# Mixing as four 64x64 products: a fused four-layer image kernel on one core

## The chip, the cores and the metric

The kernel runs on one core of one Trainium2 chip. The metric is the device time of one execution in microseconds. A core has a matrix engine (PE, with its weight loads PEld), a vector engine (DVE), a scalar engine (ACT), a general engine (POOL), and a sync engine (SP) that here only issues transfers. Each engine runs its own instructions in order; between engines there are semaphores. Products write PSUM, [...]DVE and ACT read them from there.

## The reference, cut to what matters

The input `x` holds 16 images of 64 channels of 128 x 128 pixels in fp32. Four residual layers follow each other; `_gn` is a group norm over pairs of channels.

```python
# layer 0: gram matrix of an image's channels, applied to it, then a 1x1 convolution
xf = x.reshape(B, C, N)
gram = jnp.einsum('bcn,bdn->bcd', xf, xf) / N
y = jnp.einsum('bcd,bdn->bcn', gram, xf)
out = jnp.einsum('oc,bchw->bohw', conv_w, y.reshape(B, C, H, W))

x = x + _L0_conv_ref(_gn(x), L0_conv_conv_w)
x = x + _L1_conv_ref(_gn(x))               # |3x3 gradient in x| + |3x3 gradient in y|, per channel
x = x + _L2_conv_ref(_gn(x), L2_conv_W, L2_conv_b)   # temporal shift, 3x3 convolution
x = x + _L3_conv_ref(_gn(x), ...)          # binary 3x3, then 1x1, then a batch norm over all images
```

Layer 0 is linear in the pixels once the image's gram matrix is known: its result is a 64 x 64 matrix (called `A` below, with the residual and the norms' factors in it) times the image's 64 channels, plus a constant. The batch norm of layer 3 needs sums over all 16 images, so the last step comes after everything else.

## The kernel before

**Pieces.** An image is handled in 8 chunks (`NS`), one a step. A chunk is 8 rows (`R`) of the upper half of the image and the 8 rows that lie 64 below: partitions 0 to 63 are the 64 channels of the upper half's rows, partitions 64 to 127 the channels of the lower half's. Products take 4 rows (`CP`), 512 columns, at a time.

**Stages.** `Gram` (from line 464) reads an image with its rows across partitions (`load`, tile `xr`, 512 KB each), copies them on ACT into `xw` (`rows_to_columns`), and forms the gram matrix in 128 small products into `pg`; `gram_chain` turns it, in a chain of small DVE steps and products in the PSUM tile `bank`, into `abd` (128 x 128, with `A` twice on its diagonal and zeros elsewhere) and the coefficients `co`. `Front` (from line 513) is layers 0 and 1: `load` brings a chunk of `x`, `mix` multiplies it by `abd` into the bank `po`, `prepare` normalizes it on ACT into `xh`, `sobel` does the gradients on DVE, `store` writes the result to memory (`x2_d`). `Layer2` and `Layer3` read their rows back or from tiles; each has in every step six products into `one` and two times five (`own`) into the two halves of `two`. `own` needs a difference of rows `d`, which DVE makes, and a shifted copy of it `qd`, made by ACT copies for layer 3 and by two transfers on POOL's queue for layer 2.

**Order.** Every engine's instructions are kept in the order of the program (the wrapper `InOrder`, line 63). The main loop (line 978) runs over steps, and in a step over four quarters `q`; in each quarter first layer 3, then layer 2, then `Front`, then `Gram`, each with its own image and chunk: layer 3 starts at step 35 + 8b, layer 2 at 25 + 8b, `Front` at 15 + 8b for image b. So three images are in work at a time, and a fourth one's gram. At the end of a quarter every open chain goes one link further (`tick`). PE's order in a step is thus: layer 3's `one` and first `own` (eleven products), its second `own` (five), the first mixing, layer 2's `one` and first `own` (eleven), its second `own` (five), the second mixing. The gram's 128 products stand in three blocks at the end of the quarters named in `Gram.at` and `Gram.half`.

**The fill.** The grams of images 1 to 6 run twice as fast (`half`, four steps each, from step 12 on), those of images 7 to 15 at one image for eight steps (`at`), from step 38 on. `pace` (line 939) holds the step at which each starts. `xr` has three buffers.

**Mixing.** `small_product` (line 171) makes two products of 128 x 64, one for each half of the output partitions. `mix(i, 0)` stands in the second quarter, `mix(i, 1)` in the fourth, both into the single bank of the pool `ps_po`; the bank of the pool `ps_g` holds `pg`, and at the start of an image the product `pe` of the row beyond the halves' border. A product of fp32 shows in the profile as two matmuls, its two passes.

**The end.** From step 155 on, the buffers come free one by one and are filled with the stored results; after the batch norm's sums, only transfers with one ACT and one DVE operation for each 512 KB remain.

Of the kernel before, what the change touches and what calls it, by code (L numbers as in the profile page):

```python
# [10 lines left out]
F32 = mybir.dt.float32  # L11
# [4 lines left out]
B, C, H, W = 16, 64, 128, 128  # L16
P = 128
# [3 lines left out]
R = 8  # L21
NS = HH // R
EARLY = 3
CP = 4
# [84 lines left out]
def tile_kernel(ctx: ExitStack, tc: tile.TileContext, x, cw_h, w2_t, b2, wbin_t, w1_t, b1, gamma, beta, consts, out):  # L109
    nc = tc.nc  # L110
    pe, dve, act, sp, pool = (InOrder(tc, e) for e in (nc.tensor, nc.vector, nc.scalar, nc.sync, nc.gpsimd))
# [4 lines left out]
    small = ctx.enter_context(tc.tile_pool(name="small", bufs=4))  # L116
# [19 lines left out]
    def flat(ap):  # L136
        return ap.rearrange("p j w -> p (j w)")

    def halves(d, h, r0, n):

        v = d[0:C * HW].rearrange("(c r) -> c r", r=HW)
        return v[:, (h * HH + r0) * W:(h * HH + r0 + n) * W]
# [16 lines left out]
    ps_po = ctx.enter_context(tc.tile_pool(name="ps_po", bufs=1, space=PSUM))  # L159
    ps_g = ctx.enter_context(tc.tile_pool(name="ps_g", bufs=1, space=PSUM))  # L160
# [5 lines left out]
    def cols(o):  # L166
        return slice(o * C, (o + 1) * C)

    last = [1]

    def small_product(dst, wt, src):

        for o in (1 - last[0], last[0]):
            pe.matmul(dst[cols(o)], wt[:, cols(o)], src, start=True, stop=True)
        last[0] = o


    bank = ps_sm.tile([P, 512], F32, name="bank")
# [233 lines left out]
    def gram_product(pg, w):  # L412

        s = w % 2
        pe.matmul(
            pg[s * C:(s + 1) * C, :], xw[:, w // 2, 0:C, s], xw[:, w // 2, :, s],
            start=(w < 2), stop=(w >= W - 2),
        )
        last[0] = s

    def rows_to_columns(b, m, t):
        act.copy(
            xw[:, :, m * C // 8:(m + 1) * C // 8, :].rearrange("p w c t -> p c w t"),
            t.rearrange("p c (w t) -> p c w t", t=2),
        )
# [38 lines left out]
    class Gram:  # L464
        first, last = 0, NS + 1

        def __init__(self, b):
            self.b, self.xr, self.w = b, {}, 0

        def at(self, i, q):  # L470
            b = self.b
            if i < NS:
                if q == 0 and i != 1:
                    for m in range(i + (1 if i == 2 else 2) if i else 0, min(i + 3, NS)):
                        self.load(m)

                if q == 3 and i > 0:
                    for m in (0, 1) if i == 1 else (i,):
                        rows_to_columns(b, m, self.xr.pop(m))
                return  # L480
            n = 4 * (i - NS) + q

            self.part({0: 44, 2: 42, 4: 42}.get(n, 0))
            if n == 6:
                chains.append(gram_chain(b, self.pg))

        def part(self, n):
            if self.w == 0 and n:
                self.pg = ps_g.tile([P, CP, W], F32, tag="g", name=f"pg_{self.b}")[:, 0, 0:C + 1]
            for _ in range(n):  # L490
                gram_product(self.pg, self.w)
                self.w += 1

        def load(self, m):
            t = xin.tile([P, C // 8, W], F32, tag="xr", name=f"xr_{self.b}_{m}", bufs=3)
            sp.dma_start(t, x[self.b].rearrange("c h w -> h c w")[:, m * C // 8:(m + 1) * C // 8, :])
            self.xr[m] = t

        def half(self, r):

            if self.b > 1 and 6 <= r < 6 + NS:
                rows_to_columns(self.b, r - 6, self.xr.pop(r - 6))
            if self.b > 1 and 3 <= r < 3 + NS:
                self.load(r - 3)
            self.part({14: 44, 16: 42, 18: 42}.get(r - (self.b == 1), 0))
            if r - (self.b == 1) == 19:
                chains.append(gram_chain(self.b, self.pg))


    lo, hi = slice(0, C), slice(C, P)  # L510
    coefs2, coefs3 = {}, {}

    class Front:
        first, last = -3, NS

        def __init__(self, b):
            self.b, self.xs, self.po, self.x2 = b, {}, {}, {}
            self.st = stp.tile([P, 2, NS], F32, tag="st2", name=f"st2_{b}")

        def chunk(self, i):  # L520
# [5 lines left out]
        def load(self, i):  # L526
            b = self.b
            t = xin.tile([P, R, W], F32, tag="x", name=f"x_{b}_{i}")
            for h in range(2):
                sp.dma_start(flat(t[h * C:(h + 1) * C]), halves(x[b].rearrange("c h w -> (c h w)"), h, i * R, R))  # L530
            self.xs[i] = t

        def mix(self, i, g):
            if self.b == 0 and (i, g) in ((0, 1), (1, 0)):

                po = ps_two.tile([P, 2, CP, W], F32, tag="two", name=f"po_0_{i}_{g}")[:, 0]
            else:
                po = ps_po.tile([P, CP, W], F32, tag="po", name=f"po_{self.b}_{i}_{g}")
            small_product(po, self.abd, self.xs[i][:, g * CP:(g + 1) * CP, :])
            self.po[i, g] = po  # L540
# [9 lines left out]
        def at(self, i, q):  # L550
            b = self.b
            if q == 0:
                if i == -3:

                    self.xe = xin.tile([P, W], F32, tag="xe", name=f"xe_{b}", bufs=1)
                    sp.dma_start(self.xe[lo], x[b][:, HH, :])
                    sp.dma_start(self.xe[hi], x[b][:, HH - 1, :])
                    sp.dma_start(x2_d[b][0:W].rearrange("(p w) -> p w", p=1), w0[0:1, 0:W])
                if i + 3 < NS and i + 3 not in self.xs:
                    self.load(i + 3)  # L560
                if -1 <= i < NS - 1:
                    self.prepare(i + 1, 1)
                if 1 <= i:
                    self.store(i - 1)
                    act.activation(
                        junk.rearrange("p (j w) -> p j w", w=W), self.x2.pop(i - 1), AF.Square,
                        accum_out=self.st[:, 1, i - 1:i],
                    )
                if i == NS:
                    chains.append(coefficients(self.st, lambda co: coefs2.update({b: co}), b2_sb))  # L570
            if q == 1 and -2 <= i < NS - 2:
                if i == -2:
                    self.abd, self.co = lead.pop(b)
                    self.pe = ps_g.tile([P, CP, W], F32, tag="g", name=f"pe_{b}")[:, 0, :]
                    small_product(self.pe, self.abd, self.xe)
                self.mix(i + 2, 0)
            if q == 2:
                if i == -2:
                    nc.gpsimd.memset(self.chunk(0)[lo, 0, :], 0.0)
                    self.normalized(self.chunk(0)[hi, 0, 1:1 + W], self.pe[hi], hi)  # L580
                    self.pel = small.tile([P, W], F32, tag="pel", name=f"pel_{b}", bufs=1)
                    self.normalized(self.pel[lo], self.pe[lo], lo)
                if i == NS - 2:
                    nc.gpsimd.memset(self.chunk(NS - 1)[hi, R + 1, :], 0.0)
                    act.copy(self.chunk(NS - 1)[lo, R + 1, 1:1 + W], self.pel[lo])
            if 0 <= i < NS:
                self.sobel(i, q)
            if q == 2 and -2 <= i < NS - 2:
                self.prepare(i + 2, 0)
            if q == 3 and -2 <= i < NS - 2:  # L590
                self.mix(i + 2, 1)
                self.xs.pop(i + 2)

# [98 lines left out]
    class Layer2:  # L692
        first, last = -2, NS
# [146 lines left out]
    class Layer3:  # L840
        first, last = -1, NS
# [87 lines left out]
    live = {}  # L929
# [9 lines left out]
    pace = {}  # L939
    at = 12  # L940
    for b in range(1, B):

        pace[b] = at, 2 if b <= 2 * EARLY else 1
        at += NS // pace[b][1] + (2 if b == 2 * EARLY else 0)
    last_one = NS * (B - 1) + starts[0][1]
    steps = last_one + NS + 1

# [30 lines left out]
    for step in range(starts[2][1] - 2, steps):  # L978
        for q in range(4):
            for b in range(B):  # L980

                i = step - starts[2][1] - NS * b
# [10 lines left out]
            for b in range(1, B):  # L993
                at, n = pace[b]
                if n == 1:
                    run(Gram, b, step - at, q)
                elif 0 <= step - at <= 5:
                    live.setdefault((Gram, b), Gram(b)).half(4 * (step - at) + q)
# [110 lines left out]
```

## Time and profile before

| | |
|---|---|
| median of 3 runs | 2795.21 us (2790.94 to 2795.56) |
| the profiled execution | 2793.34 us, its span 2791.6 us |
| PE, DVE, ACT, POOL busy over the span | 80%, 79%, 76%, 31% |
| mean granted PE clock | 0.900 |
| steps of an image beside a gram, from one image's first `u<-xh` to the next's | 136.8 us |
| the same without a gram | 122.7 to 124.2 us |
| moved by transfers | 685.97 MB, 246 GB/s |

The span is the time from the first to the last instruction. In the page, a line of a group gives line, engine, operation, out<-in, count, then busy time, the mean of one in ns, and the idle time of the engine before them. Nearly all instructions carry the line 73, that of the wrapper, so groups are told apart by their tiles. In a timeline a line is start, length, engine, operation, tiles, shape and count, and in brackets the idle time before it with what ended it. The ends of matmuls are modelled: they overlap, and their starts say more than their lengths. Of a matmul 128*64 means 128 rows and 64 columns of the array.

### The profile page before, as it was taken

The page shows a single profiled execution, that of the slowest core. Times are in us where ns is not written, and L with a number is a line of the kernel's source. Part 1 is how long each engine was busy: PE and PEld are TensorE (multiplying, and loading weights), DVE is VectorE, ACT ScalarE, POOL GpSimd, SP SyncE. Part 2 cuts the span into 40 slices and gives each one's busy share as a digit, 9 for nine tenths or more (in the row PEclk, how much of TensorE's full clock was granted, in tenths as well). Part 3 has the DMA queues.
Part 4 walks back from the last instruction along what each step waited for, and adds up shares of the span by engine and source line. Part 5 has one row for each costly group of instructions (what it writes and reads, how often), then busy time and mean ns, then how long its engine had stood idle before and what let it go on. Part 6 is the DMA issues. An engine that isn't in the chain of part 4 may idle for free. (4 is left out here: it accounts for less than half of the span.)

```text
span 2791.6 us, 46444 instructions
## 1 busy us (share of the span) xinstructions
PE 2232.5 (80%) x14836; PEld 1097.1 (39%) x14836; DVE 2200.6 (79%) x3751; ACT 2115.3 (76%) x3177; POOL 865.2 (31%) x1350
## 2 busy tenths in 40 slices
PE   6578899999999999999999999999999995000000
PEld 4234444534454444353534343466666641000000
DVE  4998999898989898989898989999996435333332
ACT  4666789888888888888888888998997667333332
POOL 2054434342434343334343434444444310000000
PEclk8689999999999999999999999999999997555555
DMA  7789878888888888888888867888887768999999
GB/s 193 196 224 235 223 203 237 218 228 211 222 222 219 222 221 224 221 220 220 223 219 225 215 182 198 213 205 216 208 208 185 214 194 277 419 420 420 420 420 390
DMA packets 680290, 685.97 MB, mean 246 GB/s; under 512 B 60096, under 2 KB 580448, under 8 KB 680048
## 3 DMA queue, kind: packets, MB, share of 16 engines
q1 hardware_dynamic: 654896, 613.83, 74.4%
q0 software_dynamic: 25152, 69.18, 10.1%
q8 instruction: 120, 1.97, 0.3%
q14 instruction: 122, 1.00, 0.1%
HBM read 346.23 MB, written 268.44 MB: 220 GB/s over the span
## 5 line engine op out<-in xcount | busy, mean ns | idle before, releaser
L73 PE MATMUL two<-d,w 128*64 128x508 f32 (+2 forms) x2560 | 898.7, 587 | 0.0
L73 PE MATMUL two<-d,wi 128*64 128x508 f32 (+3 forms) x1536 | 629.8, 576 | 0.0
L73 POOL DMA_DIRECT2D qd<-d x512 | 270.8, 531 | 892.5 <-issue 330.2
L73 PE MATMUL two<-qd,pk 128*64 128x512 f32 (+1 forms) x1024 | 518.6, 588 | 3.1 <-DMA qd<-d 2.4
L73 POOL TENSOR_SCALAR edges<-v,co 64x8 f32<-64x8 f32 x512 | 330.0, 645 | 355.6 <-ACT v L73 240.4
L73 PE MATMUL po<-x,abd 128*64 128x512 f32 x1024 | 385.9, 626 | 50.3 <-ACT xh L73 47.7
L73 PEld LDWEIGHTS two<-d,w 128*64 128x64 f32 x2560 | 297.4, 136 | 289.5 <-issue 219.5
L73 PE MATMUL one<-v,w 128*64 128x508 f32 (+2 forms) x1600 | 409.6, 578 | 0.0
L73 PE MATMUL one<-v,wi 128*64 128x508 f32 (+3 forms) x1536 | 408.9, 590 | 0.0
L73 DVE TENSOR_TENSOR d<-v 128x512 f32<-128x512 f32 (+1 forms) x512 | 346.0, 679 | 41.5 <-POOL v L73 16.7
L73 ACT COPY qd<-d 64x512 f32<-64x512 f32 x512 | 315.4, 616 | 21.0 <-DVE d L73 14.6
L73 ACT ACTIVATE xh<-po,co 128x128 f32<-128x128 f32 (+1 forms) x480 | 274.9, 621 | 62.4 <-PE po L73 58.9
L73 DVE SCALAR_TENSOR_TENSOR e<-e 128x1032 f32<-128x1032 f32 (+1 forms) x256 | 313.4, 1224 | 0.0
L73 DVE SCALAR_TENSOR_TENSOR y<-two,c 128x1024 f32<-128x1024 f32 x128 | 156.1, 1220 | 129.8 <-ACT v L73 71.5
L73 PEld LDWEIGHTS two<-d,wi 128*64 128x64 f32 x1536 | 196.3, 135 | 146.4 <-issue 110.7
L73 POOL TENSOR_SCALAR v<-v,kc 128x9 f32<-128x9 f32 x256 | 234.8, 930 | 11.9
L73 ACT ACTIVATE v<-x,co 128x512 f32<-128x512 f32 (+2 forms) x368 | 234.9, 705 | 0.0
L73 PEld LDWEIGHTS one<-v,w 128*64 128x64 f32 x1600 | 163.4, 137 | 178.3 <-issue 128.6
L73 PEld LDWEIGHTS one<-v,wi 128*64 128x64 f32 x1536 | 156.2, 138 | 163.0 <-issue 126.1
L73 ACT ACTIVATE u<-u 128x1024 f32<-128x1024 f32 x128 | 135.3, 1057 | 88.4 <-DVE u L73 87.0
L73 DVE SCALAR_TENSOR_TENSOR u<-xh 128x1170 f32<-128x1170 f32 x128 | 175.7, 1373 | 6.0 <-ACT xh L73 4.4
L73 PEld LDWEIGHTS two<-qd,pk 128*64 128x64 f32 x1024 | 128.6, 136 | 120.3 <-issue 81.2
(165 smaller groups left out, 3463.7 us busy)
## 6 DMA issues: line engine op xcount, KB each, us to landing
x<-in_x SPq DMA_DIRECT2D x256, 256.0 KB, 4.2
x_d<-u SPq DMA_DIRECT2D x512, 128.0 KB, 3.7
y_d<-y SPq DMA_DIRECT2D x512, 128.0 KB, 4.2
x_d<-x SPq DMA_DIRECT2D x496, 128.0 KB, 2.6
xr<-in_x SPq DMA_DIRECT2D x120, 512.0 KB, 6.0
qd<-d POOLq DMA_DIRECT2D x256, 130.0 KB, 3.0
qd<-d POOLq DMA_DIRECT2D x256, 129.8 KB, 3.6
v<-x_d SPq DMA_DIRECT2D x448, 72.1 KB, 3.0
```

The lines of the kernel that those rows point to most:

```text
L73: return self.tc.keep_in_program_order(call(*args, **kwargs))
```

## The change

From image 3 on (`four`), a chunk of `x` is laid out otherwise: partitions 0 to 63 hold the first four rows of both halves, partitions 64 to 127 the next four. Mixing is then four products of 64 x 64: group of rows g stands on partitions of half g and meets the copy of `A` in that corner of `abd`; half h of the image goes to output partitions of half h; the first group's results lie in the bank of `ps_po`, the second's in that of `ps_g`. All four stand in the second quarter. The border row's product moves to the fourth quarter of an image's first mixing step and into the `ps_po` bank, and its two ACT steps go to the next quarter. The gram of images 7 to 15 gathers in 65 columns of `bank`, since `ps_g` is taken, and starts one step earlier. In the fill, the ACT copies of rows stand in other quarters, spread over ten in place of eight, and each is followed by the request for the load that takes the buffer just read, across the end of an image too. Images 0 to 2 mix as before.

```diff
         def part(self, n):
             if self.w == 0 and n:
-                self.pg = ps_g.tile([P, CP, W], F32, tag="g", name=f"pg_{self.b}")[:, 0, 0:C + 1]
+                if self.b <= 2 * EARLY:
+                    self.pg = ps_g.tile([P, CP, W], F32, tag="g", name=f"pg_{self.b}")[:, 0, 0:C + 1]
+                else:
+                    self.pg = bank[:, 3 * P:3 * P + C + 1]
...
         def half(self, r):
-            if self.b > 1 and 6 <= r < 6 + NS:
-                rows_to_columns(self.b, r - 6, self.xr.pop(r - 6))
-            if self.b > 1 and 3 <= r < 3 + NS:
-                self.load(r - 3)
+            if self.b == 2 and r == 0:
+                for m in range(3):
+                    self.load(m)
+            m = {3: 0, 4: 1, 5: 2, 7: 3, 8: 4, 9: 5, 11: 6, 12: 7}.get(r)
+            if self.b > 1 and m is not None:
+                rows_to_columns(self.b, m, self.xr.pop(m))
+                if m + 3 < NS:
+                    self.load(m + 3)
+                elif self.b < 2 * EARLY:
+                    live.setdefault((Gram, self.b + 1), Gram(self.b + 1)).load(m + 3 - NS)
...
         def load(self, i):
             b = self.b
             t = xin.tile([P, R, W], F32, tag="x", name=f"x_{b}_{i}")
-            for h in range(2):
-                sp.dma_start(flat(t[h * C:(h + 1) * C]), halves(x[b].rearrange("c h w -> (c h w)"), h, i * R, R))
+            if self.four:
+                t = t.rearrange("p (h r) w -> p h r w", h=2)
+                v = x[b].rearrange("c (h r) w -> c h (r w)", h=2)
+                for g in range(2):
+                    j = (i * R + g * CP) * W
+                    sp.dma_start(t[cols(g)].rearrange("p h r w -> p h (r w)"), v[:, :, j:j + CP * W])
+            else:
+                for h in range(2):
+                    sp.dma_start(flat(t[h * C:(h + 1) * C]), halves(x[b].rearrange("c h w -> (c h w)"), h, i * R, R))
             self.xs[i] = t
+
+        def mix_four(self, i):
+            for g, (pool, tag) in enumerate(((ps_po, "po"), (ps_g, "g"))):
+                self.po[i, g] = pool.tile([P, CP, W], F32, tag=tag, name=f"po_{self.b}_{i}_{g}")
+            t = self.xs.pop(i)
+            order = 1 - last[0], last[0]
+            for g in range(2):
+                for h in order:
+                    pe.matmul(self.po[i, g][cols(h)], self.abd[cols(g), cols(g)], t[cols(g), h], start=True, stop=True)
...
             if q == 1 and -2 <= i < NS - 2:
                 if i == -2:
                     self.abd, self.co = lead.pop(b)
+                if i == -2 and not self.four:
                     self.pe = ps_g.tile([P, CP, W], F32, tag="g", name=f"pe_{b}")[:, 0, :]
                     small_product(self.pe, self.abd, self.xe)
-                self.mix(i + 2, 0)
+                if self.four:
+                    self.mix_four(i + 2)
+                else:
+                    self.mix(i + 2, 0)
+            if q == 3 and i == -2 and self.four:
+                self.pe = ps_po.tile([P, CP, W], F32, tag="po", name=f"pe_{b}")[:, 0, :]
+                small_product(self.pe, self.abd, self.xe)
+            if (i, q) == ((-1, 0) if self.four else (-2, 2)):
+                nc.gpsimd.memset(self.chunk(0)[lo, 0, :], 0.0)
...
-            if q == 3 and -2 <= i < NS - 2:
+            if q == 3 and -2 <= i < NS - 2 and not self.four:
                 self.mix(i + 2, 1)
                 self.xs.pop(i + 2)
...
         pace[b] = at, 2 if b <= 2 * EARLY else 1
-        at += NS // pace[b][1] + (2 if b == 2 * EARLY else 0)
+        at += NS // pace[b][1] + (1 if b == 2 * EARLY else 0)
```

More of the change, by code (lines that the diff above doesn't have):

```diff
@@ L517, in __init__ @@
             self.b, self.xs, self.po, self.x2 = b, {}, {}, {}
+            self.four = b >= EARLY
             self.st = stp.tile([P, 2, NS], F32, tag="st2", name=f"st2_{b}")
@@ L573, in at @@
                     self.abd, self.co = lead.pop(b)
+                if i == -2 and not self.four:
                     self.pe = ps_g.tile([P, CP, W], F32, tag="g", name=f"pe_{b}")[:, 0, :]
                     small_product(self.pe, self.abd, self.xe)
-                self.mix(i + 2, 0)
-            if q == 2:
[L578 to L582, printed above, removed]
+                if self.four:
[7 more added lines that the diff above has]
+                nc.gpsimd.memset(self.chunk(0)[lo, 0, :], 0.0)
+                self.normalized(self.chunk(0)[hi, 0, 1:1 + W], self.pe[hi], hi)
+                self.pel = small.tile([P, W], F32, tag="pel", name=f"pel_{b}", bufs=1)
+                self.normalized(self.pel[lo], self.pe[lo], lo)
+            if q == 2:
                 if i == NS - 2:
```

## The prediction

> **What bounds the kernel now.** I read the page from the top: busy shares, then the 40 slices, to see where which engine is full.
>
> ```profile
> PE 2232.5 (80%) x14836; PEld 1097.1 (39%) x14836; DVE 2200.6 (79%) x3751; ACT 2115.3 (76%) x3177; POOL 865.2 (31%) x1350
> PE   6578899999999999999999999999999995000000
> DVE  4998999898989898989898989999996435333332
> PEclk8689999999999999999999999999999997555555
> ```
>
> PE is full from slice 6 to slice 33, at full clock; DVE is nearly full over the same stretch and full earlier, in the fill; the last seven slices are transfers, which the change does not touch. Next I cut stretches by time, at the first `u<-xh` of an image: one image with a gram beside it, one without, and the third image of the fill.
>
> ```profile
> 1071.70:1208.50 136.80, 135.83 (x930) 57.45 (x927) 127.01 (x227) 122.06 (x191) 49.29 (x82) 1.00 0.84 219
> 1877.30:2001.50 124.20, 124.20 (x632) 79.99 (x629) 120.56 (x182) 113.72 (x182) 57.38 (x82) 1.00 0.81 209
> 252.00:393.50 141.50, 125.29 (x1082) 60.34 (x1084) 125.36 (x258) 105.07 (x161) 53.96 (x82) 0.95 0.82 213
> ```
>
> The columns are PE, PEld, DVE, ACT, POOL busy, clock, DMA share, GB/s. An image with a gram takes 136.8 us, PE stops in it once, for 0.97 us; without a gram it takes 124.2 and PE never stops. But DVE needs 127.0 and 120.6 of them. So PE is first and DVE a close second. The timeline says when DVE is second:
>
> ```profile
> 1076.15 0.38 DVE L73 TENSOR_TENSOR two<-two,edges 128x8 f32<-128x8 f32 x2 [1.96 <-PE two L73]
> 1086.53 1.23 DVE L73 SCALAR_TENSOR_TENSOR y<-two,c 128x1024 f32<-128x1024 f32 x1 [3.40 <-ACT junk L73]
> 1158.31 0.61 PE L73 MATMUL two<-qd,pk 128*64 128x512 f32 x1 [0.97 <-DMA qd<-d]
> ```
>
> DVE's idle time lies where the gram products (three blocks of 2.8 us on PE) delay the layers: 0.83 us late in the image before, 1.96 and 3.40 us here (the 3.40 ends when `own` of layer 3 is through, at 1086.3; the ACT named had long been done). From 1086.5 to about 1200 DVE idles 0.75 us in all. There PE waits once on DVE's side (the row difference `d`, copied by DMA). The time from the end of a `d` to the matmul that reads its copy falls, for layer 2's last, from 13 us beside the gram to 7.9, 8.0, 7.3 and 7.1 later; at 8.0 PE already stood still. So PE can't go further ahead of DVE than it is: in some 100 us of each such image both are the bound.
>
> **What the skill says.** The Trainium skill, "TensorE: Matmul & The Clock Gate", Part 3 (The mechanism): products on different tiles of the array run at the same time. The trace shows that for the two 64-column tiles, which start together every 0.43 us, and nothing for row halves. "TensorEngine Tiling (Array Packing)", Key Properties: "Mode switching requires drain". The trace agrees, in a product of another shape:
>
> ```profile
> 1123.78 0.59 PE L73 MATMUL two<-d,wi 128*64 128x508 f32 x1
> 1124.30 0.43 PE L73 MATMUL bank<-rw 2*128 2x64 f32 x2
> 1124.66 0.28 PE L73 MATMUL bank<-s,kc 128*64 128x2 f32 x4
> 1124.80 0.62 PE L73 MATMUL two<-d,wi 128*64 128x512 f32 x1
> 1125.26 0.59 PE L73 MATMUL two<-d,wi 128*64 128x512 f32 x1
> ```
>
> The same page, Gotcha 1 (PSUM Pressure): row tiles must write different PSUM banks; hence the second bank. "Perfetto Trace Analysis", Identifying the Most-Contended Engine: matmul busy time doesn't tell how full PE is, occupancy does for Vector. So I count PE by starts, not ends.
>
> **The change, part by part.** (1) Mixing. Now: four products a step, each two passes (x1024 over 16 images of 8 steps), two tiles at a time, 0.427 us a pass: 2 x 2 x 0.427 = 1.71 us. Then: all four at once, 2 x 0.427 = 0.85. Each visit adds two switches. From the rows above: the last pass started at 1123.78, ended streaming 0.43 later at 1124.21, the next shape started at 1124.30: 0.09. Back: second `rw` pass at 1124.46, 0.05 of streaming, next at 1124.66: 0.15. The first pass after a switch lasts 0.46 instead of 0.427, twice a visit: 0.03 to 0.05 each. Sum 0.3; a visit costs 1.15 and saves 0.56. A second cost: pairs shift against each other when an odd number (11 in layer 3's first quarter, 5 in its second) is cut by the gram's block. Today the odd one shares the array with the mixing; before a switch it runs alone, 0.43. Two of an image's eight visits follow a gram block so. PE's work falls by 8 x 0.56 - 2 x 0.43 = 3.6 us an image.
>
> What of it reaches the end? In the 100 us where DVE is full, PE only waits longer, 0. In the stretch that the gram makes PE's own, from PE's arrival at layer 2's last `own` (about 118 us into the image) to the end of DVE's last wait (14.8 into the next), PE's order holds today three half mixings, 3 x 0.854 = 2.56; then one whole, 1.15 to 1.58 with an odd one. Saved 1.0 to 1.4, say 1.2, in nine gram blocks beside images 4 to 12: 11 us. Images 13 to 15: DVE idles 1.94 us of 124.2 over waits longer than 0.15 us; of that 1.3, three times: 4. Image 3, without a gram for most of it: 129.8 us, DVE idle 3.1, gain 1. The tail (steps without mixing) keeps its time.
>
> (2) Moved: the second mixing goes from the fourth quarter to the second, so ACT's `prepare` of the next step finds it ready (its waits of 2.32 and 1.11 us beside the gram go), and SP's next `x` load isn't held for it (SP waited 63.5 us on `po`, 37 times); stores queue behind those loads and come sooner. Nothing at the end waits for either: 0. The border row's product stays a few small passes (0.22 us an image), its two ACT steps the same length; its new wait, for ACT's first `prepare`, is the one that the second mixing had there; behind it on PE stands layer 3, as now. The second bank is freed by the ACT step that frees `po` today: no later. Gram in the shared bank from the eighth image: same products, its first waits for ACT's copy as now. Gram a step earlier: SP's loads, ACT's copies and the chain's small DVE operations move with it, past the same neighbours: 0.
>
> (3) `x` loads in 2 KB runs instead of 4 KB: today's 4,096-byte packets take 0.254 us. Bounds: same time a byte, 0; same time a packet, 128 more packets a step, 128 x 0.254 / 16 = 2.0 us of each DMA engine's 16, share 0.84 to 0.96. I take 0: 16 packets of 2,048 bytes on POOL's queue took 0.135 each.
>
> (4) Fill. A load used to be asked for three quarters before its copy, now four or more, the first three during the gram before. In the third image:
>
> ```profile
> 260.45 1.20 ACT L73 COPY xw<-xr 128x1024 f32<-128x1024 f32 x1 [3.87 <-DMA xr<-in_x]
> 265.41 1.15 ACT L73 COPY xw<-xr 128x1024 f32<-128x1024 f32 x1 [2.53 <-DMA xr<-in_x]
> 267.54 1.29 DVE L73 SCALAR_TENSOR_TENSOR u<-xh,co,u 128x1024 f32<-128x1024 f32 x1 [5.67 <-ACT u L73]
> ```
>
> ACT waited 6.4 us for rows, behind it stood the absolute values, and DVE, the fill's bound, lost 5.67. I count 5: the first gram of this form asks for three loads at once with its first copy three quarters later (6 us to land, some 8 there), which can cost 1 or 2; at worst the whole gain is lost, at best 6.
>
> Sum: 11 + 4 + 1 + 5 = 21 us. The profiled execution took 2793.3 us (span 2791.6), 1.9 under the median 2795.2: 2772 in its terms, 2774 as a median.
>
> **Rivals.** *Row halves do not run at once* (four 64x64 products in fp32 have no row in this trace). A visit costs 1.71 + 0.3: PE grows by 8 x 0.3 + 2 x 0.43, about 3 us an image where PE is first. Nine images at 3, three at 2, less 5 of the fill: 2823. It turns the sign as soon as a visit costs more than 1.71, that is when switches and odd ones take 0.86 instead of 0.3. For it: nothing shown. Against: two column tiles do overlap fully, and the banks differ. *PE stays the bound*: if PE may go further ahead of DVE than 7 us (the copies' DMA is short with DMA free), the whole 3.6 counts: 9 x 3.6 + 0.97 each, 4 of the last three, 6 of the fill: near 2745. Against: margins flat from 35 us into an image on, and DVE's 127.0 plus its small gaps make some 129.5. *Nothing moves*: the gain beside the gram is taken by odd passes and the larger number of DMA packets, and the fill's wait comes back at another load: 2790 to 2800.
>
> **How the numbers follow.** Forecast 0.54 (2760 to 2788), PE stays the bound 0.14, nothing moves 0.15, row halves in turn 0.12, another loss from transfers 0.05. A measurement of this kernel tells about 0.2% (5.6 us) from no change. Faster by more: 0.68; within: 0.15; slower: 0.17. The range, 2750 to 2802, holds the forecast, most of "nothing moves" and the near part of the second; the likeliest's own is 2760 to 2788.
>
> **What would show it.** Right: mixing's eight passes start in two groups of four 0.43 us apart, next start 1.15 after; PE idle appears in images with a gram, some 2 to 3 us waiting on `d` or its copies; images without a gram at 122 to 123; DVE's waits beside the gram shorter by about 1.2; no copy waiting for rows near 260 us. Wrong: mixing's passes two at a time; an image still without idle PE and shorter by 4 us; or DVE waiting longer beside the gram.

## The result, and the profile after

The changed kernel takes 2798.99 us (median of 12 executions, 2793.24 to 2805.0), the kernel before, on the same chip, 2794.22 us (median of 12, 2790.94 to 2795.93). The ratio is 1.0018, 95% interval 1.0010 to 1.0027: 5 us longer where 21 us less were forecast. The profiled execution took 2796.47 us, its span is 2794.7 us.

The page after, busy shares:

```profile
PE 2217.1 (79%) x14836; PEld 935.2 (33%) x14836; DVE 2200.8 (79%) x3751; ACT 2115.4 (76%) x3177; POOL 890.8 (32%) x1350
```

PE is busy for 15 us less, and the span is no shorter. The windows, cut as before at the first `u<-xh` of an image (an image with a gram, one without, the third of the fill):

```profile
1077.20:1215.00 137.80, 135.51 (x926) 55.36 (x924) 126.98 (x227) 122.02 (x191) 52.14 (x82) 1.00 0.84 218
1883.60:2006.00 122.40, 120.21 (x632) 42.44 (x630) 120.25 (x181) 113.09 (x181) 59.06 (x82) 1.00 0.84 211
253.20:389.60 136.40, 125.07 (x1098) 60.57 (x1096) 125.62 (x258) 103.33 (x159) 56.41 (x82) 0.97 0.83 216
```

The image without a gram and the fill went as forecast: 124.2 to 122.4 and 141.5 to 136.4 us. The image with a gram grew from 136.8 to 137.8, though mixing is cheap now. DVE is busy for as long as before in it (127.0 us), so its idle time grew by as much, from 9.8 to 10.8. From the timeline of PE in that image:

```profile
1150.84 1.09 PE L73 MATMUL po<-x,abd 64*64 64x512 f32 x8
1151.86 2.79 PE L73 MATMUL one<-v,wi 128*64 128x512 f32 x12
```

Eight passes, and the next product starts 1.02 us after the first of them. By the starts in the trace they come as two groups of four (0 to 0.02 us, 0.48 to 0.50), so all four products do run at once; with the 0.09 us before it a visit costs 1.11. Added up by starts over the image (the first matmul of one kind to the first of the next), mixing fell from 13.7 to 8.2 us. But the products of layers 2 and 3, the same ones as before, rose from 111.3 to 115.6 us, the gram's and the small products from 10.8 to 11.8, and PE's idle time from 1.0 to 2.2.

Two groups of the page, PE's products into `one` of a layer-3 chunk and DVE's row differences, before and then after:

```profile
L73 PE MATMUL one<-v,w 128*64 128x508 f32 (+2 forms) x1600 | 409.6, 578 | 0.0
...
L73 DVE TENSOR_TENSOR d<-v 128x512 f32<-128x512 f32 (+1 forms) x512 | 346.0, 679 | 41.5 <-POOL v L73 16.7
```

```profile
L73 PE MATMUL one<-v,w 128*64 128x508 f32 (+2 forms) x1600 | 387.2, 589 | 27.3 <-ACT c L73 27.3
...
L73 DVE TENSOR_TENSOR d<-v 128x512 f32<-128x512 f32 (+1 forms) x512 | 345.8, 678 | 60.7 <-issue 25.3
```

The first had no idle time ahead of it before; now 27.3 us, about 2 in most images from the fourth on. The second's idle time rose from 41.5 to 60.7. DVE's waits of the image at 1077.2, from its timeline:

```profile
1193.19 0.69 DVE L73 TENSOR_TENSOR d<-v 128x512 f32<-128x512 f32 x1 [1.46 <-issue]
1198.30 0.39 DVE L73 TENSOR_TENSOR two<-two,edges 128x8 f32<-128x8 f32 x2 [1.98 <-PE two L73]
1208.08 1.22 DVE L73 SCALAR_TENSOR_TENSOR y<-two,c 128x1024 f32<-128x1024 f32 x1 [2.88 <-ACT junk L73]
1214.38 0.69 DVE L73 TENSOR_TENSOR d<-v 128x512 f32<-128x512 f32 x1 [1.33 <-issue]
```

They still lie beside the gram, and add to 7.65 us here (6.19 before, with 0.83 + 1.96 + 3.40). The waits of 1.96 and 3.40 became 1.98 and 2.88; those of `d` are new. A likely reason, by the order of the program, is that the buffer of `d` is read by layer 2's `own`, which stands behind the whole mixing now; no run tests it. The time that PE needs from the start of layer 2's last `own` before the gram to the end of layer 3's second `own` behind its third block fell from some 33.6 us to 33.2 to 33.4, by 0.3 where 1.2 were forecast.

In the fill, ACT's copies no longer wait for rows to land. All waits over 0.5 us ahead of copies from `xr` in its timeline up to 330 us, each ended by the gram's products (`pg`) and none by a transfer:

```profile
70.84 1.20 ACT L73 COPY xw<-xr 128x1024 f32<-128x1024 f32 x1 [3.79 <-PE pg L73]
222.53 1.20 ACT L73 COPY xw<-xr 128x1024 f32<-128x1024 f32 x1 [1.11 <-PE pg L73]
282.92 1.21 ACT L73 COPY xw<-xr 128x1024 f32<-128x1024 f32 x1 [0.58 <-PE pg L73]
```

The first `u<-xh` of image 3 starts at 389.6 us instead of 393.5.

### The profile page after: what moved, and what is told of

Read it like the earlier page. It is cut to its first block, busy times and chain, and to the rows that moved or that the text cites. A ratio compares the mean times of both kernels' runs of the same rounds, so it can differ in the third digit from the quotient of the medians.

```text
span 2794.7 us, 46308 instructions
## 1 busy us (share of the span) xinstructions
PE 2217.1 (79%) x14836; PEld 935.2 (33%) x14836; DVE 2200.8 (79%) x3751; ACT 2115.4 (76%) x3177; POOL 890.8 (32%) x1350
## 3 DMA queue, kind: packets, MB, share of 16 engines
q14 instruction: 123, 1.01, 0.1%
## 5 line engine op out<-in xcount | busy, mean ns | idle before, releaser
L73 PE MATMUL two<-d,w 128*64 128x508 f32 (+2 forms) x2560 | 875.1, 586 | 0.0
L73 PE MATMUL two<-d,wi 128*64 128x508 f32 (+3 forms) x1536 | 604.1, 576 | 0.0
L73 POOL TENSOR_SCALAR edges<-v,co 64x8 f32<-64x8 f32 x512 | 346.2, 676 | 328.9 <-ACT v L73 200.8
L73 PE MATMUL one<-v,w 128*64 128x508 f32 (+2 forms) x1600 | 387.2, 589 | 27.3 <-ACT c L73 27.3
L73 DVE TENSOR_TENSOR d<-v 128x512 f32<-128x512 f32 (+1 forms) x512 | 345.8, 678 | 60.7 <-issue 25.3
L73 PEld LDWEIGHTS two<-d,w 128*64 128x64 f32 x2560 | 278.7, 136 | 306.4 <-issue 269.7
L73 PE MATMUL one<-v,wi 128*64 128x508 f32 (+3 forms) x1536 | 357.5, 596 | 0.3 <-ACT c L73 0.3
L73 PE MATMUL po<-x,abd 64*64 64x512 f32 (+1 forms) x1024 | 184.2, 642 | 40.8 <-ACT xh L73 38.6
L73 PEld LDWEIGHTS one<-v,w 128*64 128x64 f32 x1600 | 136.7, 138 | 219.7 <-issue 136.5
L73 PEld LDWEIGHTS one<-v,wi 128*64 128x64 f32 x1536 | 109.2, 138 | 220.9 <-issue 210.2
L73 ACT ACTIVATE v<-v,co 128x1154 f32<-128x1154 f32 x128 | 172.0, 1344 | 4.4 <-DMA v<-x_d 4.4
```

Source lines behind the costliest of these rows:

```text
L73: return self.tc.keep_in_program_order(call(*args, **kwargs))
```

## The experiments

**Theory 1.** A product that is left over when an odd number stands ahead of a switch of the tile mode (from products of 128 x 64 to those of 64 x 64) runs alone, and the forecast counted too few of these. **Theory 2.** The gram's move by a step costs about 1 us an image, whatever the mixing. **Theory 3.** The whole mixing in the second quarter stands ahead of layer 2's products, and DVE waits for those. A fourth, on the clock, came from the traces of the first runs. Every run has its own executions of the kernel before beside it, medians 2793.7 to 2794.6 us.

### The fill alone

The kernel before with the `half` of the change.

> The kernel before with the changed fill alone (row copies spread, loads asked for early). All theories: image 2's first step loses its 5.67 us wait, the first step of image 3 starts some 4 us earlier, and nothing later changes. 2789 to 2791 us, 4 to 5 us below the kernel before.

2789.86 us, ratio 0.9987 (0.9981 to 0.9994): 4.0 us less. The fill is what it was meant to be; all later images keep their 136.8 us.

### The gram's move alone

The kernel before with

```diff
+                if self.b <= 2 * EARLY: ...
+                else:
+                    self.pg = bank[:, 3 * P:3 * P + C + 1]
...
-        at += NS // pace[b][1] + (2 if b == 2 * EARLY else 0)
+        at += NS // pace[b][1] + (1 if b == 2 * EARLY else 0)
```

> The kernel before with the gram's sums in the shared bank and the gram one step earlier, mixing and fill as before. Theory 1 (single products before the mode switches eat the gain of mixing): the shift alone costs nothing that lasts, image 3 is some 6 us longer and image 12 some 6 us shorter, total 2793 to 2796 us. Theory 2 (the shifted gram itself costs about 1 us in each image that has one): gram images at 137.8 us instead of 136.8, total 2801 to 2804 us.

2796.66 us, ratio 1.0009 (1.0002 to 1.0015): 2.8 us more. Gram images take 137.2 to 137.3 us (one 137.7), between what the two theories say: the move costs 0.4 to 0.5 us an image, without any change to the mixing. It is real, and too small to be the whole.

### The changed kernel with the gram at its old step

```diff
-        at += NS // pace[b][1] + (1 if b == 2 * EARLY else 0)
+        at += NS // pace[b][1] + (2 if b == 2 * EARLY else 0)
```

> The changed kernel with the gram put back to the step where the kernel before has it; mixing as four products and the changed fill stay. Theory 1 (single products eat the gain): gram images stay at 137.5 to 138 us, total 2797 to 2801 us. Theory 2 (the shift by a step costs 1 us an image): gram images at 136.8 us or less, total 2788 to 2791 us.

2793.75 us, ratio 1.0002 (0.9994 to 1.0010): 5.2 less than the changed kernel, and a miss of both theories' ranges. But 3.9 more than the fill alone, which differs from it in the mixing (and the bank) only. So with the gram where it was the four products still lose. Gram images fall into two kinds, 137.2 and 138.9 to 139.3 us; the fourth theory is about the second kind.

### The gram's blocks at even places

The changed kernel with

```diff
-            self.part({0: 44, 2: 42, 4: 42}.get(n, 0))
+            self.part({1: 44, 3: 42, 5: 42}.get(n, 0))
```

Layer 3 puts eleven products into the first quarter and five into the second, layer 2 the same into the third and fourth. So the ends of the first and third quarters stand behind an odd number, those of the second and fourth behind sixteen and thirty-two.

> The changed kernel with the gram's three blocks at the ends of the second, fourth and again the second quarter instead of the first, third and first; block sizes the same. Theory 1 (odd splits of the products leave single ones before the mode switches, 0.43 us each): fewer visits have a single product ahead of them, gram images shorter by 1 to 2 us, total 2784 to 2790 us. Theory 2 (the shift) and theory 3 (the whole mixing in the second quarter stands ahead of layer 2's products, for which VectorE waits): no gain, 2797 to 2803 us.

2783.29 us, ratio 0.9963 (0.9950 to 0.9975): 15.7 us less than the changed kernel. A part of this may be the clock's (below): this profile has one stretch at half rate after the fill, that of the changed kernel four. Window of one image:

```profile
1208.80:1344.90 136.10, 133.69 (x924) 53.62 (x922) 127.00 (x226) 121.78 (x191) 53.91 (x82) 1.00 0.87 222
```

I count as lone a pass of 381 columns or more that has no other such pass, nor one of mixing, starting within 0.40 us. A gram image of the kernel before has 3 to 5, one of the changed kernel 17 or 18, six or seven of them between 103 and 131 us, where the gram stands; here 10 or 11, none of them there. They stand where DVE is the bound. One lone product in the changed kernel, ahead of the mixing at 109 us of the image at 1077.2:

```profile
1184.93 1.86 PE L73 MATMUL two<-d,w 128*64 128x508 f32 x6
1186.72 1.09 PE L73 MATMUL po<-x,abd 64*64 64x512 f32 x8
```

Six passes are three products. Run two at a time they would take three times 0.43 us; up to the mixing it is 1.79, four times 0.43 and the switch.

### The same places with the old mixing

The kernel before with the diff above.

> The kernel before, with the gram's three blocks at the ends of the second, fourth and again the second quarter; mixing, fill and gram step as before. If odd splits of the products hurt only the four-way mixing, nothing is won: 2793 to 2796 us. If the gram's own blocks, which stand behind an odd number of products too, pay the same 0.43 us for a product that runs alone, up to two of three blocks an image are cheaper: 4 to 8 us, 2786 to 2790 us.

2793.26 us, ratio 0.9999 (0.9991 to 1.0007): nothing won. With the two-pass mixing, which has the layers' own tile shape, the odd product shares the array with the mixing. The places matter only to the four-way mixing.

### The changed kernel without the four products

```diff
-            self.four = b >= EARLY
+            self.four = False
```

> The changed kernel with mixing as before (two passes in two quarters) in every image; the gram's shift and bank and the changed fill stay. If the parts add up (fill 4 us less, gram shift 3 us more): 2792 to 2794 us, so that the four products alone cost 5 to 7 us. If the four products do not cost anything and the loss comes from the shift in company with the fill: 2797 to 2801 us.

2793.23 us, ratio 0.9997 (0.9989 to 1.0005). The parts add up: fill 4.0 less, gram's move 3.4 more (against the fill alone), and the four products 5.8 us more, all at odd places.

### The wait of 2 us, and the clock

In the changed kernel's profile most gram images take 137.8 us, but images 9 and 10 take 139.3. The trace shows one difference. PE's timeline, the same product in images 8 and 9:

```profile
1161.18 2.78 PE L73 MATMUL one<-v,w 128*64 128x512 f32 x12 [0.75 <-ACT c L73]
...
1299.02 4.48 PE L73 MATMUL one<-v,w 128*64 128x512 f32 x12 [2.15 <-ACT c L73]
```

In image 8 PE's idle time is in two pieces (1.29, and 0.75 here), in image 9 in one of 2.15, and the same twelve passes take 1.7 us longer. The windows of 4 us from 1161.2 and 1298.8 have the granted clock in the eighth place:

```profile
1161.20:1165.20 4.00, 4.00 (x20) 1.44 (x22) 4.00 (x6) 3.93 (x7) 1.09 (x2) 1.00 0.43 83
1298.80:1302.80 4.00, 3.78 (x10) 1.17 (x12) 4.00 (x6) 3.94 (x7) 1.20 (x3) 0.57 0.37 71
```

Starts lie 0.85 us apart instead of 0.43 until 1302.2. The Trainium skill, "TensorE: Matmul & The Clock Gate", Part 1 (The HAM clock gate), says that the array's clock goes to half after an idle window of about 3.4 us, and that the window runs freely, whatever the kernel does. The half rate and its length of 3.41 us agree, and so does the free-running window: in all 16 traces every change of the granted clock, the first one apart, lies on a grid of 3.413 us (456.23 and 1299.32, two starts of half rate in this one, are 247 such steps apart). The wait needed does not agree: here waits of 1.94 to 2.37 us were followed by half rate in four images of ten (3, 9, 10, 12), and waits as long in other images were not. What tells them apart is how the wait lies on the grid. Two neighbouring steps of it around image 9's wait, then two around image 5's, of 2.27 us up to 747.91:

```profile
1295.91:1299.32 3.41, 1.26 (x8) 0.28 (x6) 3.41 (x6) 3.41 (x7) 2.92 (x3) 1.00 0.36 92
1299.32:1302.73 3.41, 3.41 (x10) 0.98 (x8) 3.41 (x5) 3.35 (x6) 1.08 (x2) 0.50 0.40 77
```

```profile
742.96:746.37 3.41, 2.68 (x14) 0.68 (x10) 3.41 (x6) 3.26 (x5) 3.10 (x6) 1.00 0.61 180
746.37:749.78 3.41, 1.87 (x10) 0.73 (x12) 3.41 (x6) 3.37 (x6) 1.45 (x1) 1.00 0.51 131
```

Image 9's wait falls into one step, in which PE is busy for 1.26 us of 3.41, and the next step is at half rate. Image 5's is shared by two steps, and nothing follows. From 325 to 1980 us of all 16 traces, 11 steps have PE idle for 2.03 us or more, and each is followed by half rate; 12 have it idle for 1.90 to 2.00, and one is (the 1.94 of image 10); of those with less, none is. So in this stretch the border lies near 2.0 us of idle time in a step, far from a whole one; in the fill it is less sharp, between some 1.7 and 2.0. The test, in the changed kernel:

```diff
+                if i == 1 and 2 <= b <= 10:
+                    for _ in range(10):
+                        for o in (1 - last[0], last[0]):
+                            pe.matmul(bank[cols(o), 449:512], w3[:, 2, 1, cols(o)], k("I")[:, 0:63], start=True, stop=True)
                 shared(one, w3[:, 2], t)
```

> The changed kernel with ten pairs of small products (63 columns, written to unused columns of the shared bank, read by nobody) ahead of the layer-3 product that in each image from the fourth on waits some 2 us for ScalarE's copy of the last one's result. Theory 4: the faster mixing lets TensorE run dry there, and a wait of 2 us in one piece makes the granted clock fall to about half for the next 3.4 us (0.57 in the window of image 9's, against 1.00 in image 8's), 1.5 us lost each time it happens, at 4 images of 10 in the profile. Then the small products keep the clock up, no stretch at half rate is left there, and the time falls by 3 to 6 us and spreads less: 2793 to 2796 us. If the half rate has another cause, the time stays at 2797 to 2801 us or rises by the small products' own time.

2794.54 us, ratio 1.0003 (0.9995 to 1.0011): 4.5 us less than the changed kernel, in a range of 4.0 us instead of 11.8. Image 9's stretch in this run, timeline and window:

```profile
1298.35 1.35 PE L73 MATMUL bank<-kc,w 128*64 128x63 f32 x40
1300.67 2.78 PE L73 MATMUL one<-v,w 128*64 128x512 f32 x12 [0.96 <-ACT c L73]
```

```profile
1300.60:1304.60 4.00, 3.93 (x20) 1.38 (x22) 4.00 (x5) 3.94 (x7) 1.09 (x2) 1.00 0.36 73
```

Forty small passes halve the wait, the clock stays at 1.00, and none of these products ran at half rate after the fill. So by this run 4.5 of the 5.8 us of the four products come by the clock. The other 1.3 are a sum: in the profiles a gram image without half rate is still 0.5 us longer than with the old mixing (137.8 against 137.3 us), and the images without a gram are shorter.

### Even places and the old step

The changed kernel with the blocks at even places and the gram at its old step.

> The changed kernel with the gram's blocks at the ends of the second, fourth and again the second quarter, and the gram at the step where the kernel before has it. If the cost of the shift by one step (5 us with the blocks at the first quarter's end) is one of place, whatever the quarter: 2777 to 2780 us. If it came from the odd splits or from VectorE's wait behind the mixing in the same step, which the other quarters have changed: 2782 to 2785 us, as with the shift.

2779.76 us, ratio 0.9951 (0.9939 to 0.9964): 3.5 less than with the move. The move costs about what it did with the old mixing (2.8 alone, 3.4 with the fill), so it is a matter of its own.

### The control: even places, the fill, old mixing

The kernel before with the even places and the change's `half`.

> The kernel before with the even blocks and the changed fill, mixing in two passes, gram at its old step: the base without its four products. If the parts add up, 2789 to 2790 us, and the four products with even splits are worth 9 to 10 us; if they do not, the gain of the base has another source than the mixing, and this run lies nearer to 2780 us.

2789.66 us, ratio 0.9984 (0.9978 to 0.9991), as the sum says. The windows of one gram image of each, first this run, then the one above:

```profile
929.90:1066.60 136.70, 135.69 (x924) 56.01 (x922) 126.92 (x226) 121.76 (x191) 54.96 (x82) 1.00 0.84 220
```

```profile
1064.70:1200.50 135.80, 133.33 (x925) 54.16 (x922) 126.91 (x226) 121.88 (x191) 53.76 (x82) 1.00 0.85 222
```

The four products, with even places and the gram at its step, are worth 0.9 us a gram image and 9.9 us in all. With odd places, at the same step, they lost 3.9.

### The mixing one product later, and two

This takes theory 1 without moving the gram. Base: the run with even places and the old step. `issue` counts products and calls the mixing behind the first one, or the second, of those that follow its quarter:

```diff
-                    self.mix_four(i + 2)
+                    behind[0] = 1, lambda: self.mix_four(i + 2)        # 2 in the twin
...
             last[0] = o
+            if behind[0]:
+                left, mixing = behind[0]
+                behind[0] = (left - 1, mixing) if left > 1 else None
+                if left == 1:
+                    mixing()
```

> Base: the kernel of the run with even blocks and the old gram step (2779.8 us). The four products of the mixing are issued one product later, behind the first product of layer 2's next group, so that an odd number of 128x64 products stands on both sides of most visits; all else as in the base. Theory 1 (a product left over before a switch of the tile mode runs alone, 0.43 us, and so does the one after it): about ten more lone products an image, 4.3 us of TensorE, of which the stretch beside the gram pays two thirds or more: 2800 to 2820 us. Theory 3 (what counts is how early or late the mixing stands before layer 2's products): no more than the twin run with two products, 2775 to 2785 us.

> As the twin, but the mixing is issued two products later, so that the number on both sides stays even. Theory 1: as the base, 2778 to 2783 us. Theory 3: two products of layer 2 come 1 us earlier, and VectorE behind them; 2772 to 2778 us.

One later: 2789.97 us, ratio 0.9988 (0.9981 to 0.9994). Two later: 2777.76 us, ratio 0.9943 (0.9928 to 0.9958), the fastest kernel of this study. PE's timelines around one visit, the odd run, then the even one:

```profile
1150.12 1.05 PE L73 MATMUL one<-v,wi 128*64 128x512 f32 x2
1151.09 1.09 PE L73 MATMUL po<-x,abd 64*64 64x512 f32 x8
```

```profile
1141.40 1.08 PE L73 MATMUL one<-v,wi 128*64 128x512 f32 x4
1142.41 1.09 PE L73 MATMUL po<-x,abd 64*64 64x512 f32 x8
```

From the first pass to the mixing it is 0.97 us for two passes, one product, and 1.01 us for four, two products: the lone one costs as much as a pair. Windows of an image:

```profile
1071.80:1209.10 137.30, 135.28 (x926) 55.58 (x924) 126.94 (x227) 122.01 (x191) 52.95 (x82) 1.00 0.84 221
```

```profile
1063.70:1199.70 136.00, 133.45 (x926) 53.84 (x924) 127.00 (x227) 121.94 (x191) 53.58 (x82) 1.00 0.85 222
```

The Trainium skill, "TensorEngine Tiling (Array Packing)", Key Properties, says that a switch of mode drains the array; these lines show what the drain costs when one of the two column tiles has nothing left to do. Lone passes in an image: 19 and 9. Ten passes are five products, 5 x 0.43 = 2.2 us; the image differs by 1.3, the whole by 12.2 us. One product later costs 10.2 us over the base and two products later nothing: it is the odd number that counts, and this much of theory 1 is shown. Its price was set too high, the odd run was expected 20 us or more over the base. Theory 3 expected both runs to be like each other, and falls as the main cause. The even run lies 2.0 us under the base, with overlapping ranges, just under what theory 1 gave for it and inside theory 3's range; its gram images take what the base's take, 135.9 against 135.8. Its profile has no half rate after the fill, the base's has three stretches.

### Small products in the even kernel

The even places and the old step, with the small products of the clock's test where PE waits there (images 4 to 12, and 13 to 15).

> The base (even blocks, old gram step) with ten pairs of small products ahead of the layer-3 product that waits some 2 us once an image, images 4 to 12 and 13 to 15, as in the run that kept TensorE busy. If the half rate after the wait is what is left of theory 4 (two or three images of 13 in the base's profile): 2 to 5 us less, 2775 to 2778 us. If not: 2779 to 2781 us.

2779.60 us, ratio 0.9949 (0.9937 to 0.9962), 0.2 under the base: a miss. The profile has no half rate left after the fill, and image 9 takes 136.2 us instead of 137.6; but that was the only one of the base's profile that lost time to it (in images 12 and 14 there was half rate at no cost), and the medians don't show it. So there was less to win here than in the changed kernel, some 1.8 us in that one execution; why the medians show nothing of it isn't settled.

### What in the gram's move costs: the bank or the step

The kernel before with the bank alone, and with the gram one step later instead of earlier (3 for 2 in the last diff line).

> The kernel before with the gram's sums in the shared bank, at the old step. If the step costs the 3 us: as before, 2793 to 2795 us, gram images at 136.8 us. If the bank costs them (small products and sums in one bank): 2796 to 2798 us, gram images at 137.2 us.

> The kernel before with the gram one step later. If the cost of a place goes by which step's other work the blocks meet, the image's time changes by some tenths of a us either way: 2788 to 2800 us, with gram images at another value than 136.8 us. If the step is indifferent, gram images stay at 136.8 us, and the total at 2793 to 2795 us.

The bank: 2793.87 us, ratio 0.9998 (0.9990 to 1.0006), nothing. The later step: 2788.91 us, ratio 0.9982 (0.9974 to 0.9989), some 5 us less (5.6 by the medians). Windows of one gram image, one step earlier, then one step later:

```profile
939.90:1077.10 137.20, 136.21 (x926) 73.69 (x924) 127.23 (x227) 122.00 (x191) 49.52 (x82) 1.00 0.86 218
```

```profile
1068.20:1204.50 136.30, 135.69 (x924) 69.19 (x922) 127.10 (x226) 121.69 (x191) 47.68 (x82) 1.00 0.85 222
```

So the place in the order of steps is worth 0.4 to 0.5 us an image in either direction. Which neighbour makes the difference stays open. The later step together with the even four-way mixing wasn't tried.

## Why the prediction was wrong

By its own steps:

- **What bounds the kernel** held: PE where the gram stands, PE and DVE elsewhere.
- **Four at once**: right, 1.11 us a visit against 1.15 forecast. With even places and the gram at its step the four products were worth 9.9 us, of the 16 that the forecast gave to all but the fill. The 2 KB runs cost nothing measurable: a packet of 2,048 bytes took 0.124 us in the gram image, one of 4,096 bytes 0.245 before (0.254 in the prediction), so the time went by the byte; DMA share 0.84 before and after, an `x` load lands in 4.1 us against 4.2.
- **"Saved 1.0 to 1.4, say 1.2, in nine gram blocks"**: failed, and with it 11 of the 21 us. Behind it stands **"Two of an image's eight visits follow a gram block so"**. Five of eight visits had a product alone ahead of them: the two behind a gram block, and three behind the small products of the chains (24, 41 and 57 us into the image), which I had not counted. In front of the gram's two blocks at odd places a product ran alone as well. In the stretch that the gram makes PE's own, four products ran alone (at 103, 109, 115 and 130 us of image 8), where the kernel before has one. Three more are 3 x 0.43 = 1.3 us of the 2.56 - 1.11 = 1.45 that mixing saves there, which leaves 0.2; PE's stretch shows 0.2 to 0.4.
- **"DVE's waits beside the gram shorter by about 1.2"**: failed, they grew by 1.5 us (6.19 to 7.65), which the prediction had named as a sign of being wrong. The new waits are those for `d`, 1.46 and 1.33 us. About 0.45 us of the image's 1.0 comes by the gram's move; what the waits for `d` cost by themselves was not tried.
- **"In the 100 us where DVE is full, PE only waits longer, 0"**: failed. PE's idle time came, as long as forecast (2 to 3 us; 2.23 in image 8), but most of it waits for ACT's copy `c` and not for `d`. Where it is one piece, as in most images, and falls into one step of the clock's grid, it drops the clock to half for 3.4 us, and then PE is late where it is the bound. 4.5 us by the run that kept PE busy. The forecast took the clock of 1.00 for granted.
- **"Gram a step earlier ... 0"**: failed. 2.8 us alone; 3.4, 3.5 and 5.2 in company; the step, not the bank.
- **Images 13 to 15: 4**: 2.6 in the profiles (355.0 to 352.5 us, from image 13's first `u<-xh` to image 15's last), size off.
- **Fill: 5**: 4.0.

The measured sum is -4.0 + 3.4 + 5.8 = 5.2 us, where the two kernels differ by 4.8. That the measured 2799 us lies inside 2750 to 2802 is luck as far as the forecast goes: it lies there by the rival "nothing moves", which gave 2790 to 2800 and the odd passes as a reason. That part was right; the transfers and the fill in it were not, and the clock and the gram's move were in no rival.

## What to carry to other kernels

A product in another tile mode is a wall in PE's order: count what stands on both sides of it, and put it where the pairs come out even; an odd one costs as much as a pair. When an engine gets faster than the one it works with, its saved time becomes waits, and here a wait of some 2 us in one piece on PE, more than half a step of the clock's grid, cost some 1.5 us where the half rate struck, and the mixing had won 0.3 in PE's stretch; price the wait, not only the work. A block moved by one step meets other neighbours: a move at equal work is not a cost of zero until it is run.

## What was not expected of the hardware

Half rate of PE lasted 3.41 us at a time (starts 0.85 us apart instead of 0.43) and began on a fixed grid of 3.413 us. From image 3 on it followed every step of this grid in which PE was idle for 2.03 to 2.55 us, and once one with 1.94; twelve steps with 1.90 to 2.00 us were followed by it this once, steps with less never. Four fp32 products of 64x64 run at once, in two groups of passes 0.48 us apart. A lone 128x64 fp32 product ahead of a switch takes 0.97 us up to the next mode's start, two take 1.01.
